# Turning q and k with VectorE and ScalarE in place of TensorE, 96x96 gram products among the convolutions, and a rotated order of attention's output channels

## The chip, the cores and the metric

The kernel runs on one core of a Trainium2 chip. The metric is device time in microseconds (us), from the first to the last instruction of the slowest core; here there is one core. The engines are TensorE (PE, matmuls, with its weight loads shown apart as PEld), VectorE (DVE), ScalarE (ACT), GpSimd (POOL) and SyncE (SP), which only issues transfers. Each engine works through its own queue in order, and semaphores make one wait for another. SBUF is the on-chip memory with 128 partitions; PSUM holds what TensorE writes, in banks.

## The reference

Two layers work on an image x of 384 channels and 192x192 pixels, in float32. The second (a 7x7 depthwise convolution after a group normalization) isn't touched by the change. The first is this, cut to what matters:

```
x1  = groupnorm(x)                                  # 32 groups
qkv = max over 2x2 pixels of (w_qkv @ x1 + b_qkv)   # 1152 channels, 96x96
qkv = depthwise 3x3 of qkv + b_dw
q, k, v = the three thirds, each as 8 heads of 48 channels x 9216 pixels
q, k = q, k divided by their norm over the pixels
attn = q @ k^T * temperature                        # 48x48 for each head
out  = sum over i of topk_softmax(attn, k_i) @ v * a_i,  k_i = 24, 32, 36, 38
x    = x + (w_proj @ upsample2x2(gelu(out)) + b_proj)
```

The attention is over channels: one 48x48 matrix for each head. Both q @ k^T (a sum over all pixels) and attn @ v are therefore products in which only the blocks of one head on the diagonal count.

## The kernel before

The channels lie on the partitions, in three tiles of 128 (`KT` = 3). A head has `HC` = 48 channels, so heads cross the borders of the tiles.

The q/k stage (lines 551 to 763) goes through the image in `NB` = 24 blocks of `PR` = 4 pooled rows. For each block and each of the six channel tiles of q and k, `pooled` multiplies the weights `wq` with the loaded rows (three groups of 512 columns, three matmuls of depth 128 each, L639) into one of the four PSUM buffers "pq", and VectorE takes the maximum over 2x2 pixels (L647) into a ring of rows, `ring`. `bordered` lets ScalarE copy a row of the ring to its other end (L669, L673), in two of three blocks. One block later, `depthwise` makes the 3x3 convolution with nine VectorE instructions (L680, L682) into a buffer `dst` of the pool `qkp`.

When all six tiles of a block are there, `products` (L688) does three things. ScalarE squares each tile and sums it into `ssq` (L691). TensorE transposes q and k, 128 pixels at a time, into the PSUM buffers "tr" (L700), because the sum over pixels needs pixels on the partitions, and ScalarE copies the result to SBUF as `qkT` (L706). TensorE then multiplies the turned q with the turned k into `grams`, one PSUM bank that collects the sum over all blocks (L709). `SPAN` says which columns of k meet the 128 q channels of a tile: 144, 192 and 144.

An fp32 matmul is two passes over the array, and the profile shows each pass with its weight load; a transpose is one pass.

What is between the q/k stage and the v stage: in the loop's last turn (`b == NB`) the first of 16 batches of v is convolved already (`convolve`, L530 to L549, PSUM buffers "pv"), with an `issue_after(multiplied)` that puts it behind a block's last gram product. Then `attention` (L769) scales the gram by the norms (L789), moves the heads' blocks with ten small transfers into `att` (L797), ranks and mixes the softmaxes on VectorE, spreads the result as blocks into `diag` (L851), transposes it and copies it to `attnT` (L862). Two further batches of v are convolved meanwhile.

The v stage runs over batches of 2 x 6 rows. For each, `attend` (L951) multiplies `attnT` with v: for each half and each tile `ct` of output channels, the tiles `dt` of v channels that share a head with it (`near`), seven products in all (L961), and ScalarE applies Gelu. `project` (L977) multiplies with `wp` (L985), whose rows are the channels of `gl` in the same order.

The order of instructions: the code is traced, and a planner puts each engine's queue in order, in order of the trace among those which its cost estimates hold ready. `keep(...)` fixes an instruction behind the last kept one of its engine; `issue_after(x)` puts what is traced inside it behind x on x's engine. A pool with `bufs=n` gives n buffers for each tag; a new tile waits until the old one's readers are done.

Of the kernel before, what the change touches and what calls it, by code (L numbers as in the profile page):

```python
# [8 lines left out]
F32 = mybir.dt.float32  # L9
AF = mybir.ActivationFunctionType  # L10
ALU = mybir.AluOpType
AX = mybir.AxisListType

P = 128
C = 384
KT = C // P
# [5 lines left out]
HC = C // HEADS  # L22
# [4 lines left out]
NB = PS // PR  # L27
IR = 2 * PR
BLK = IR * HW
PB = PR * PS  # L30
SUB = BLK // 512
NX = 3
GN_EPS = 1e-5


SPAN = []
for _mt in range(KT):
    _lo = (_mt * P) // HC * HC
    _hi = ((_mt + 1) * P - 1) // HC * HC + HC
    SPAN.append((_lo, _hi))  # L40

PIECES = []
for _mt in range(KT):
# [29 lines left out]
UT = 2  # L73
# [5 lines left out]
def conv_preact_d2(  # L79
# [17 lines left out]
    nc = tc.nc  # L97
# [16 lines left out]
    ident = const.tile([P, P], F32, name="ident")  # L114
# [31 lines left out]
    wp = const.tile([P, KT, C], F32, name="wp")  # L146
# [79 lines left out]

    ssq = const.tile([P, 2 * KT, NB], F32, name="ssq")
    attnT = const.tile([P, KT, C], F32, name="attnT")


    bctx = ExitStack()
# [26 lines left out]

    psx = ExitStack()
    pgram = psx.enter_context(tc.tile_pool(name="pgram", bufs=1, space=PSUM))  # L260
    gram = []
    for mt, (lo, hi) in enumerate(SPAN):
        o = sum(h - l for l, h in SPAN[:mt])
        gram.append((o, o + hi - lo))
    grams = pgram.tile([P, gram[-1][1]], F32, name="grams")
    gram = [grams[:, lo:hi] for lo, hi in gram]
    ptr = psx.enter_context(tc.tile_pool(name="ptr", bufs=3, space=PSUM))
    qx = ExitStack()
    pq = qx.enter_context(tc.tile_pool(name="pq", bufs=4, space=PSUM))
# [216 lines left out]
        w = wq[:, TWO, i * C : (i + 1) * C]  # L486
        nc.scalar.mul(w, w, rstd0[:, TWO : TWO + 1])
    with tc.issue_after(loaded):
        nc.sync.dma_start(wp, wprojT.rearrange("(t p) o -> p t o", p=P))

# [57 lines left out]

    with ExitStack() as bx:
        padp = bx.enter_context(tc.tile_pool(name="padp", bufs=1))
        qkp = bx.enter_context(tc.tile_pool(name="qkp", bufs=9))
        trp = bx.enter_context(tc.tile_pool(name="trp", bufs=2))

        gwp = bx.enter_context(tc.tile_pool(name="gwp", bufs=1))

# [66 lines left out]
        for ct in range(2 * KT):  # L624
            ring.append(padp.tile([P, 3 * PR + 2, PS + 2], F32, name=f"ring{ct}"))

        def pooled(b, ct, xb):
            rows = xb.rearrange("p t (r c) -> p t r c", c=HW)
            t = ring[ct]
            r0 = 1 + b % 3 * PR  # L630
            for g in range(3):
                begun, there = sums_qk.pop((b, ct, g), (None, False))
                ps = begun
                if not there:
                    ps = pq.tile([P, 512], F32, name=f"pq{b}_{ct}_{g}", tag="pq")
                    if begun is not None:
                        nc.scalar.copy(ps, begun)
                for kt in range(KT) if begun is None else (TWO,):
                    nc.tensor.matmul(  # L639
                        ps,  # L640
                        wq[:, kt, ct * P : (ct + 1) * P],
                        rows[:, kt, :, g * 64 : (g + 1) * 64],
                        start=(kt == 0),
                        stop=(kt == KT - 1),
                        skip_group_check=begun is not None,
                    )
                nc.vector.tensor_reduce(  # L647
                    t[:, r0 : r0 + PR, 1 + g * 32 : 1 + (g + 1) * 32],
                    ps.rearrange("p (h a w b) -> p h w a b", h=PR, a=2, b=2),
                    AX.XY,  # L650
                    ALU.max,
                )
# [32 lines left out]
            r0 = b % 3 * PR  # L685
            taps(dst, ct, lambda i, j: ring[ct][:, r0 + i : r0 + i + PR, j : j + PS])

        def products(b, qk):  # L688
            for i in range(2 * KT):
                junk = trp.tile([P, PB], F32, name=f"junk{b}_{i}", tag="junk")  # L690
                nc.scalar.activation(  # L691
                    junk, qk[i].rearrange("p h w -> p (h w)"), AF.Square,
                    accum_out=ssq[:, i, b : b + 1],
                )
            for j in range(PB // P):
                sides = []
                for s in range(2):
                    ps = ptr.tile([P, C], F32, name=f"tr{b}_{j}_{s}", tag="tr")
                    for i in range(KT):
                        nc.tensor.transpose(  # L700
                            ps[:, i * P : (i + 1) * P],
                            qk[s * KT + i].rearrange("p h w -> p (h w)")[:, j * P : (j + 1) * P],
                            ident,
                        )
                    sb = trp.tile([P, C], F32, name=f"qkT{b}_{j}_{s}", tag=f"qkT{s}")
                    nc.scalar.copy(sb, ps)  # L706
                    sides.append(sb)
                for mt, (lo, hi) in enumerate(SPAN):
                    last = nc.tensor.matmul(  # L709
                        gram[mt],  # L710
                        sides[0][:, mt * P : (mt + 1) * P],
                        sides[1][:, lo:hi],
                        start=False,
                        stop=(b == NB - 1 and j == PB // P - 1),
                        skip_group_check=True,
                    ).ins
            return last


        nc.tensor.matmul(  # L720
            grams, z[:, RUN : RUN + P], z[:, RUN : RUN + grams.shape[1]], start=True, stop=False,
            skip_group_check=True,
        )
        for b in range(NB + 1):
            xb = None
            if b < NB:
                xb = held.pop(b) if b in held else load_x(b, "xq")
            else:

                qx.close()  # L730
                pv = psx.enter_context(tc.tile_pool(name="pv", bufs=2, space=PSUM))
                xb = xpool.tile([P, 2 * UT, KT, RB * HW], F32, name="xv_begun", tag="xb")
                for kt in range(KT):
                    nc.sync.dma_start(xb[:, :, kt], image_rows(kt, order[0], 0, 2 * UT))
            qk = []
            for ct in range(2 * KT + 1):
                if b < NB and ct < 2 * KT:
                    if b == 0 and ct < 2:

                        if ct == 0:  # L740
                            pooled(b, 0, xb)
                            pooled(b, 1, xb)
                            biases()
                    else:
                        pooled(b, ct, xb)
                    bordered(b, ct)
                if b > 0 and ct > 0:
                    dst = qkp.tile([P, PR, PS], F32, name=f"qk{b}_{ct}", tag="qk")
                    qk.append(dst)
                    depthwise(b - 1, ct - 1, dst)  # L750
                    if ct == 2 * KT:
                        multiplied = products(b - 1, qk)
                    if b == NB:
                        with tc.issue_after(multiplied):
                            for n in ((), (), (0, 1), (), (2, 3), (4,), (5,))[ct]:
                                t0 = n // KT * UT
                                convolve(0, t0, n % KT, xb[:, t0 : t0 + UT], lambda ins: ins)
            if b == 2:
                for tiles in vrows:
                    row_borders(tiles)  # L760
            if b < len(pieces):
                with tc.issue_after(stats0):
                    weights(*pieces[b])

    xctx.close()

    near = {}

    def attention(ap):  # L769

# [13 lines left out]
        along_free(rkb, rn[:, KT : 2 * KT], ptr, "rk", "tr")  # L784
        yield

        scaled = ap.tile([P, KT, C // 2], F32, name="scaled")
        for mt, (lo, hi) in enumerate(SPAN):
            nc.vector.scalar_tensor_tensor(  # L789
                scaled[:, mt, 0 : hi - lo], gram[mt], rn[:, mt : mt + 1], rkb[:, lo:hi],  # L790
                ALU.mult, ALU.mult,
            )
        att = ap.tile([P, KT, HC], F32, name="att")
        for i, (mt, r0, r1, h) in enumerate(PIECES):
            eng = (nc.gpsimd, nc.scalar)[i % 2]
            o = h * HC - SPAN[mt][0]
            eng.dma_start(att[r0:r1, mt, :], scaled[r0:r1, mt, o : o + HC])  # L797
        yield


# [50 lines left out]
            eng.dma_start(diag[r0:r1, mt, h * HC : (h + 1) * HC], mix[r0:r1, mt, :])  # L851
        yield
        for dt in range(KT):
            cts = [ct for ct in range(KT) if SPAN[ct][0] < (dt + 1) * P and SPAN[ct][1] > dt * P]
            near[dt] = cts
            ps = ptr.tile([P, C], F32, name=f"aT{dt}", tag="tr")
            for ct in cts:
                nc.tensor.transpose(
                    ps[:, ct * P : (ct + 1) * P], diag[:, ct, dt * P : (dt + 1) * P], ident
                )  # L860
            lo, hi = cts[0] * P, (cts[-1] + 1) * P
            nc.vector.tensor_copy(attnT[:, dt, lo:hi], ps[:, lo:hi])  # L862

# [85 lines left out]
    def attend(i, pin=lambda ins: ins):  # L951
        b = order[i % NBC]
        vb = [vbs.pop((i, ct)).rearrange("p t c -> p (t c)") for ct in range(KT)]
        gl = gp.tile([P, KT, PBC], F32, name=f"gl{b}", tag="gl")
        for h in range(2):
            for ct in range(KT):
                dts = [dt for dt in range(KT) if ct in near[dt]]
                ps = ptr.tile([P, C], F32, name=f"po{b}_{ct}_{h}", tag="tr")
                for dt in dts:
                    keep(  # L960
# [563 lines left out]
```

## Time and profile before

| What | Value |
|---|---|
| Median of three runs | 2817.3 us (2817.22 to 2821.58) |
| Profiled execution | 2802.07 us, span 2800.4 us |
| TensorE clock granted, mean | 0.994 of full speed |
| Instructions on TensorE / VectorE / ScalarE / GpSimd | 8717 / 3383 / 1638 / 884 |
| Image moments and the first partial products | to about 190 us |
| q/k stage | to about 1355 us |
| Change of stage, attention | to about 1488 us |
| v stage | to about 2195 us |
| 7x7 convolution and output | to the end |

The profile is one execution. In a row of a group, the line number is followed by engine, operation and tiles (output <- inputs), the shapes, the count, then the total of busy time and the mean ns of one, and at the end the idle time of the engine just before these instructions, with what ended it. In a timeline row the first number is the start and the second how long the run of equal instructions lasted. In a table of stretches, each engine's busy us are followed by its count of instructions.

### The profile page before, as it was taken

Reading aid. Unit: us, or ns where it says so; the run is one execution under the profiler, and the core shown is the slowest. Engines: PE = TensorE matmul, PEld = TensorE weight load, DVE = VectorE, ACT = ScalarE, POOL = GpSimd, SP = SyncE. Lnnn points to the kernel's source line nnn. Section 1 sums busy time; section 2 is a strip of 40 time slices with the busy share of each in tenths; the row PEclk is TensorE's granted clock in tenths of the full one; section 3 lists DMA queues with packets and bytes.
Section 4 is the critical chain, followed back from the end, with each engine's and each line's share of the span. In section 5 each row is a group of like instructions: output and inputs, shape, how many; then the busy total and the mean of one; then the engine's idle time right before and its main releaser. Section 6 shows DMA issues by size and latency. Waiting matters only on the chain. (4 is left out here: it accounts for less than half of the span.)

```text
span 2800.4 us, 25638 instructions
## 1 busy us (share of the span) xinstructions
PE 2646.0 (94%) x8717; PEld 1588.6 (57%) x8717; DVE 2324.8 (83%) x3383; ACT 873.3 (31%) x1638; POOL 748.0 (27%) x884
## 2 busy tenths in 40 slices
PE   0399999999999999999999999999999899999998
PEld 0144444445445444444556666666666677777776
DVE  7989887887878878878798988889889678887786
ACT  0141111111111111111202232222323577777776
POOL 1023443100000000000102231010101477877777
PEclk9999999999999999999999999999999999999999
DMA  9976666401001001010235998575664899999998
GB/s 381 400 248 216 227 203 219 165 34 68 34 34 68 34 35 67 34 62 7 78 127 174 334 379 314 171 249 196 209 236 152 321 341 360 374 367 370 367 376 265
DMA packets 234002, 580.98 MB, mean 207 GB/s; under 512 B 16608, under 2 KB 165712, under 8 KB 217104
## 3 DMA queue, kind: packets, MB, share of 16 engines
q1 hardware_dynamic: 173376, 283.44, 28.8%
q0 software_dynamic: 37376, 148.85, 15.2%
q10 hardware_dynamic: 23120, 147.07, 14.0%
q8 instruction: 69, 1.13, 0.2%
q14 instruction: 61, 0.50, 0.0%
HBM read 370.93 MB, written 208.21 MB: 207 GB/s over the span
## 5 line engine op out<-in xcount | busy, mean ns | idle before, releaser
L639 PE MATMUL pq<-xq,wq 128*128 128x512 f32 x2268 | 990.7, 593 | 0.0
L639 PEld LDWEIGHTS pq<-xq,wq 128*128 128x128 f32 x2268 | 423.9, 190 | 491.3 <-issue 446.5
L682 DVE SCALAR_TENSOR_TENSOR qk<-ring,wd,qk 128x384 f32<-128x384 f32 x1152 | 674.8, 613 | 20.9 <-ACT ring L669 7.1
L537 PE MATMUL pv<-xv,wq 128*128 128x384 f32 x1656 | 539.8, 487 | 2.5 <-DVE rows L543 1.4
L647 DVE TENSOR_REDUCE ring<-pq 128x128 f32<-128x512 f32 x428 | 293.9, 688 | 193.5 <-PE pq L639 192.0
L1428 PE MATMUL pc<-main,w 128*128 128x288 f32 x1536 | 436.2, 407 | 3.9 <-POOL aux L1348 1.7
L537 PEld LDWEIGHTS pv<-xv,wq 128*128 128x128 f32 x1656 | 314.8, 190 | 218.6 <-DVE rows L543 3.0
L1448 DVE TENSOR_SCALAR apart<-pc,rb 32x576 f32<-32x576 f32 x384 | 312.2, 813 | 108.9 <-PE pc L1428 97.1
L1428 PEld LDWEIGHTS pc<-main,w 128*128 128x128 f32 x1536 | 290.8, 190 | 87.3 <-issue 2.1
L1446 ACT ACTIVATE apart<-pc,rb 32x576 f32<-32x576 f32 x384 | 281.1, 732 | 137.2 <-PE pc L1428 132.4
L905 DVE SCALAR_TENSOR_TENSOR vb<-rows,wd,vb 128x576 f32<-128x576 f32 x384 | 313.2, 817 | 11.2
L1428 PE MATMUL pc<-aux,h 128*128 128x288 f32 x768 | 249.5, 407 | 3.1 <-issue 2.4
L691 ACT ACTIVATE junk<-qk 128x384 f32<-128x384 f32 x144 | 75.3, 523 | 544.0 <-DVE qk L682 544.0
L1387 POOL COPY res<-apart 128x1152 f32<-128x1152 f32 (+1 forms) x96 | 218.4, 2305 | 48.6 <-DMA out_dram<-res 40.2
L773 POOL TENSOR_TENSOR rn<-rn,halfpos 128x6 f32<-128x6 f32 x1 | 1.4, 1360 | 850.6 <-DVE rn L772 850.6
L1022 DVE TENSOR_TENSOR sx<-xr,y 128x576 f32<-128x576 f32 x180 | 203.7, 1173 | 26.9 <-ACT y L993 21.2
L1063 POOL DMA_DIRECT2D sd<-sx x96 | 72.2, 755 | 491.8 <-DVE sx L1022 472.6
L543 DVE TENSOR_REDUCE rows<-pv 128x192 f32<-128x768 f32 x144 | 137.8, 957 | 55.7 <-PE pv L537 55.6
L1428 PEld LDWEIGHTS pc<-aux,h 128*128 128x128 f32 x768 | 145.6, 190 | 45.2 <-issue 4.4
L1042 ACT ACTIVATE wq<-sx,negmid 128x1152 f32<-128x1152 f32 x96 | 120.6, 1256 | 95.4 <-DVE sx L1022 91.2
L1271 DVE SCALAR_TENSOR_TENSOR w<-eye,sb,w 128x512 f32<-128x512 f32 x96 | 144.1, 1540 | 1.5
L985 PE MATMUL pr<-gl,wp 128*128 128x288 f32 x576 | 142.6, 407 | 0.0
(226 smaller groups left out, 2113.6 us busy)
## 6 DMA issues: line engine op xcount, KB each, us to landing
sd<-sx POOLq DMA_DIRECT2D x96, 600.0 KB, 9.9
out_dram<-res SPq DMA_DIRECT2D x192, 288.0 KB, 10.7
main<-sd ACTq DMA_DIRECT2D x46, 1200.0 KB, 5.1
xv<-in_x_dram SPq DMA_DIRECT2D x138, 384.0 KB, 6.5
xr<-in_x_dram SPq DMA_DIRECT2D x45, 1152.0 KB, 12.0
xq<-in_x_dram SPq DMA_DIRECT2D x21, 2304.0 KB, 8.2
w<-wt ACTq DMA_DIRECT2D x46, 1024.0 KB, 6.9
xs<-in_x_dram SPq DMA_DIRECT2D x24, 1536.0 KB, 15.6
```

Of the source, the lines that this page charges most:

```text
L537: nc.tensor.matmul(ps[:, u, 0 : RB * HW], wq[:, kt, o : o + P], xb[:, u, kt, :], start=(kt == 0), stop=(kt == KT - 1),)
L639: nc.tensor.matmul(ps, wq[:, kt, ct * P : (ct + 1) * P], rows[:, kt, :, g * 64 : (g + 1) * 64], start=(kt == 0), stop=(kt == KT - 1), skip ...
L647: nc.vector.tensor_reduce(t[:, r0 : r0 + PR, 1 + g * 32 : 1 + (g + 1) * 32], ps.rearrange("p (h a w b) -> p h w a b", h=PR, a=2, b=2), AX. ...
L682: nc.vector.scalar_tensor_tensor(dst, src, w, dst, ALU.mult, ALU.add)
L905: pin(nc.vector.scalar_tensor_tensor(dst, src, w, dst, ALU.mult, ALU.add))
L985: nc.tensor.matmul(ps[:, 0:H], wp[:, ct, ot * P : (ot + 1) * P], gl[:, ct, h * H : (h + 1) * H], start=(ct == 0), stop=(ct == KT - 1),)
L1022: nc.vector.tensor_tensor(bass.AP(flat.tensor, flat.offset + at(e) + a * RUN, [flat.ap[0], [JP, NT], [1, NJ], [at(f) - at(e), 2]],), xq[:, ...
L1271: nc.vector.scalar_tensor_tensor(mid, eye.unsqueeze(1).to_broadcast([P, 4, P]), sb[:, c : c + 1], mid, ALU.mult, ALU.add,)
L1387: keep(copy(res[ps, k], apart[ps, :, k].rearrange("p e n -> p n e")))
L1428: nc.tensor.matmul(ahead[q][:, k, 0 : NT * NJ], lhs, rhs, start=(j == 0), stop=(j == 2), skip_group_check=True,)
L1446: keep(nc.scalar.mul(dst, src, scale))
L1448: keep(nc.vector.tensor_scalar_mul(dst, src, scale))
```

## The change

In the q/k stage, each tile that `depthwise` has finished is transposed by VectorE in squares of 32x32, in place in the grid of squares (`nc.vector.transpose`, 128x384, into `turns`). When the three tiles of q (or of k) are there, ScalarE puts the squares in their places: `turned` makes 16 copies for each side, from one quadrant of 32 partitions to another, 32x288 elements each; two of four rounds are traced at once and the other two after the next tile's transpose. The squares for the norms write their unused output to a "tr" buffer in PSUM.

The gram is made of pairs of heads: four products of 96x96 for each 128 pixels, twelve a block. They are traced one after each convolution product (`pinned`, `between`): the products of block b-2 begin with channel tile 3 of block b, and from block 2 on the convolution products are kept in the written order. In the loop's last turn they stand among the first products of v, and those of the last block follow when all else is traced. `qkp` goes from 9 to 5 buffers, `trp` from 2 to 1.

In `attention`, one multiplication of 96x384 scales the gram by k's norms, and after the small transfers another, 128x144, scales it by q's.

For v, the output channels of attention are rotated by 96 (`TURN`): tile 0 holds channels 96 to 223, tile 1 channels 224 to 351, tile 2 channels 352 to 383 and 0 to 95. Each tile then shares heads with two tiles of v (`MEET`), six products where there were seven. `attnT` is cleared at the start, since only the heads' blocks are copied into it, and `wp` is loaded in the rotated order with three transfers.

```diff
+PAIR = 2 * HC
+TURN = PAIR
+MEET = [[dt for dt in range(KT) if any(
+    (TURN + ct * P + j) % C // HC in range(dt * P // HC, ((dt + 1) * P - 1) // HC + 1)
+    for j in range(P))] for ct in range(KT)]
...
+    nc.gpsimd.memset(attnT, 0.0)
...
-        nc.sync.dma_start(wp, wprojT.rearrange("(t p) o -> p t o", p=P))
+        nc.sync.dma_start(wp[:, 0:whole], ...)
+        nc.sync.dma_start(wp[0:over, whole], wprojT[C - over :])
+        nc.sync.dma_start(wp[over:P, whole], wprojT[0:TURN])
...
-        qkp = bx.enter_context(tc.tile_pool(name="qkp", bufs=9))
-        trp = bx.enter_context(tc.tile_pool(name="trp", bufs=2))
+        qkp = bx.enter_context(tc.tile_pool(name="qkp", bufs=5))
+        trp = bx.enter_context(tc.tile_pool(name="trp", bufs=1))
...
+        def pinned(ins):
+            if ins.ins.engine != mybir.EngineType.PE:
+                return ins
+            keep(ins)
+            while between and next(between[0], between) is between:
+                between.pop(0)
+            return ins
...
+                    if b > 1:
+                        pinned(ins)
...
+        def squares(b, ct, t):
+            junk = ptr.tile([P, C], F32, name=f"junk{b}_{ct}", tag="tr")
+            nc.scalar.activation(junk, t, AF.Square, accum_out=ssq[:, ct, b : b + 1])
+
+        def turned(side, turns):
+            for a in range(P // Q):
+                for f in range(P // Q):
+                    nc.scalar.copy(
+                        side[f * Q : (f + 1) * Q].rearrange("p c (t n) -> p t c n", n=P)[
+                            :, :, :, a * Q : (a + 1) * Q
+                        ],
+                        turns[a * Q : (a + 1) * Q].rearrange("p t (c n) -> p t c n", n=P)[
+                            :, :, :, f * Q : (f + 1) * Q
+                        ],
+                    )
+                yield
...
-                    for i in range(KT):
-                        nc.tensor.transpose(
...
-                    nc.scalar.copy(sb, ps)
...
+                for lo in range(0, C, PAIR):
+                    multiplied = keep(
+                        nc.tensor.matmul(
+                            grams[0:PAIR, lo : lo + PAIR],
+                            sides[0][:, j, lo : lo + PAIR],
+                            sides[1][:, j, lo : lo + PAIR],
...
+                if ct == (KT if b < NB else 1) and done:
+                    between.append(products(b - 2, done))
...
                     depthwise(b - 1, ct - 1, dst)
...
+                    nc.vector.transpose(turns[:, t], flat)
+                    squares(b - 1, ct - 1, flat)
+                    for _ in copies:
+                        pass
+                    if t == KT - 1:
+                        side = trp.tile([P, PB // P, C], F32, name=f"qkT{b}_{s}", tag=f"qkT{s}")
+                        sides.append(side)
+                        copies = turned(side, turns)
+                        for _ in range(2):
+                            next(copies)
                     if b == NB:
-                        with tc.issue_after(multiplied):
...
+                            convolve(0, t0, n % KT, xb[:, t0 : t0 + UT], pinned)
+                        if ct == 2 * KT:
+                            for _ in copies:
+                                pass
+                            between.append(products(b - 1, sides))
+                            for left in between:
+                                for _ in left:
+                                    pass
...
-            nc.vector.scalar_tensor_tensor(
-                scaled[:, mt, 0 : hi - lo], gram[mt], rn[:, mt : mt + 1], rkb[:, lo:hi],
+        nc.vector.tensor_tensor(scaled[0:PAIR], grams[0:PAIR], rkb[0:PAIR], ALU.mult)
...
+            for l, h in ((lo, min(hi, TURN)), (max(lo, TURN), hi)):
+                if l < h:
+                    o = (l - TURN) % C
+                    nc.vector.tensor_copy(attnT[:, dt, o : o + h - l], ps[:, l:h])
...
-                dts = [dt for dt in range(KT) if ct in near[dt]]
+                dts = MEET[ct]
```

## The prediction

> **What bounds the kernel now.** I first read the busy shares, then the busy time by stage, because the whole-run shares mix four stages with different limits.
>
> ```profile
> PE 2646.0 (94%) x8717; PEld 1588.6 (57%) x8717; DVE 2324.8 (83%) x3383; ACT 873.3 (31%) x1638; POOL 748.0 (27%) x884
> ```
>
> ```profile
> core 0: us, PE busy (x) PEld busy (x) DVE busy (x) ACT busy (x) POOL busy (x), PEclk, DMA share, GB/s
> 300.00:1300.00 1000.00, 998.96 (x2802) 481.22 (x2801) 802.29 (x1407) 144.55 (x432) 94.33 (x151) 1.00 0.24 87
> 1355.00:1393.00 38.00, 35.93 (x159) 24.12 (x158) 24.50 (x47) 9.13 (x26) 4.96 (x6) 1.00 0.28 94
> 1500.00:2130.00 630.00, 628.85 (x2149) 408.61 (x2148) 554.66 (x639) 174.56 (x381) 96.95 (x130) 1.00 0.72 251
> 2130.00:2200.00 70.00, 59.32 (x224) 43.60 (x223) 62.68 (x67) 36.80 (x86) 14.48 (x20) 0.91 0.73 259
> ```
>
> In the q/k stage (300 to 1300) and in the v stage (1500 to 2130) TensorE is busy 99.8% of the time. VectorE is at 80% and 88%, ScalarE at 14% and 28%, and the DMA engines have room. So the stages that the change touches are paced by TensorE. The chain of work that ended last says nothing here: it names only the output stage.
>
> Next come the groups of the q/k stage and TensorE's own timeline around one block of four rows, where starts can be subtracted (a "busy" time includes the modelled drain of each matmul).
>
> ```profile
> L682 DVE SCALAR_TENSOR_TENSOR qk<-ring,wd,qk 128x384 f32<-128x384 f32 x937 | 551.7, 614 | 19.5 <-ACT ring L669 7.1
> L647 DVE TENSOR_REDUCE ring<-pq 128x128 f32<-128x512 f32 x354 | 243.9, 689 | 177.7 <-PE pq L639 176.4
> L706 ACT COPY qkT<-tr 128x384 f32<-128x384 f32 x114 | 52.5, 477 | 118.7 <-PE tr L700 99.4 <-PE grams L709 17.4
> ```
>
> ```profile
> 1304.48 1.50 PE L700 MATMUL tr<-ident,qk 128*128 128x128 f32 x10
> 1305.82 1.02 PE L639 MATMUL pq<-xq,wq 128*128 128x512 f32 x2
> ...
> 1308.95 1.79 PE L709 MATMUL grams<-qkT,qkT 128*128 128x144 f32 x12
> 1310.58 0.49 PE L700 MATMUL tr<-ident,qk 128*128 128x128 f32 x3
> 1310.90 1.02 PE L639 MATMUL pq<-xq,wq 128*128 128x512 f32 x2
> 1311.76 1.01 PE L709 MATMUL grams<-qkT,qkT 128*128 128x144 f32 x6
> 1312.61 43.08 PE L639 MATMUL pq<-xq,wq 128*128 128x512 f32 x100
> 1355.53 2.15 PE L700 MATMUL tr<-ident,qk 128*128 128x128 f32 x13
> ```
>
> The reader sees one full block, 1304.48 to 1355.53, 51.05 us. A convolution pass (an fp32 matmul is two passes) takes 42.92/100 = 0.429 us; 108 of them make 46.35 us. What is left, 4.69 us, is 18 transposes (0.107 each where they run in threes, 2.21 us in all) and 18 gram passes (1.63 + 0.85 = 2.48 us). VectorE waits for TensorE (176 us before its reduces), not the other way round.
>
> For the v stage the same view gives the price of an attention pass: 28 of them from 1538.92 to 1545.71, 0.2425 us each.
>
> ```profile
> 1538.92 6.95 PE L961 MATMUL po<-vb,attnT 128*128 128x288 f32 x28
> 1545.71 11.78 PE L537 MATMUL pv<-xv,wq 128*128 128x384 f32 x36
> ```
>
> **What the Trainium skill says.** "TensorE: Matmul & The Clock Gate", section "LDWEIGHTS (loading the stationary operand)": the load time goes with the number of weight columns, P/1.2 ns, whatever the depth. The trace agrees for 128 columns: the 30 one-column bias passes (176.71 to 179.98) take 0.109 us each, against 0.107. By that, 96 columns load in an estimated 0.080 us. "VectorE: DVE Perf Modes", section "The three transpose paths": VectorE turns 32x32 squares only, 311 ns for 128x128 bf16. "ScalarE: Activation LUTs", section "What ACT_TABLE_LOAD costs": a ScalarE instruction with immediates takes 186 ns + 0.833 ns per element, and neighbours overlap by 93 ns. The trace agrees roughly: 96-element copies take 272 ns (266 by the page), 384-element copies from PSUM 477 ns (506).
>
> **The change part by part.**
> *TensorE, q/k.* Per block 18 transposes go: 2.21 us. The gram becomes 12 products of 96x96 in place of 9 of 128x144 or 128x192: 24 passes. Moving 96 columns costs 96/512 x 0.429 = 0.081 us a pass, 0.161 a product, and its own weights load in the same 0.080 us. The 128-column weights of the convolution pass that follows need 0.109 us beside a 0.081 us pass, so 0.028 us may show: 0.19 us a product, 2.3 us a block. Bounds: 1.93 (all loads hidden, as they are between transposes and convolutions now) and 4.6 (both loads exposed at the 190 ns of a weight-load row). I take 2.3: saving 4.69 - 2.30 = 2.39 us a block. 22 blocks' grams lie ahead of the end of the last q/k convolution: 22 x 2.39 = 52.6 us.
>
> *VectorE, q/k.* Six transposes of 128x384 a block. No row shows one. The skill's 311 ns for 128 elements plus 256 more at the 0.96 GHz of the same page is an estimated 0.58 us; without that fixed part, the 0.49 us of the one-input row L680; above, twice the estimate if fp32 ran at half rate, 1.15 us. I take 0.58: 3.5 us a block. VectorE now works 0.802 x 51.05 = 41.0 us a block; 44.5 of a new period of 48.7 us. It is hidden under TensorE with 4 us to spare; the four "pq" buffers give about 10 us of slack in order.
>
> *ScalarE, q/k.* Six copies of 477 ns go; 32 copies of 32x288 come, 426 ns by the page (333 from start to start), 10.7 to 13.6 us a block. The squares stay, writing to PSUM. From 7.4 us now, ScalarE goes to some 18 of 48.7 us. Hidden. Behind these copies in its queue stand the squares, which free the "qk" buffers (five, 40 us of taps), and the ring-row copies of L669/L673, which VectorE needs one channel tile later; a copy ahead of them delays them by 0.4 us each, and VectorE has waited only 7 us for them in 1000.
>
> *The new wait.* Convolution products now stand in written order, and each product of block b-2 stands between two of them, from channel tile 3 of block b. The first waits for the last ScalarE copies of block b-2's k side. Taps end some 6 us into block b, 16 copies take 5.3 us: ready at about +12, wanted at +24. Cost nothing; half a block covers it. Queued behind it are all convolutions, and behind these VectorE's reduces. Single buffers of the turned sides: the next q side is written after the last product, some 13 us into ct 3; ScalarE waits, nobody behind it is urgent.
>
> *The end of the stage.* From the last q/k convolution (1355.53) to the first convolution of the second v batch (1392.99) is 37.5 us now. After it: k side of block 22 ready at +9 (taps 3, transpose 0.6, copies 5.3), until which TensorE idles behind its first product; then 72 v passes of 0.3225 us and 12 products, 25.5 us: +34. VectorE's rest (15.5 us of taps now, some 5 us of lead that it no longer builds up, 2 us of transposes, 5 of reduces) ends near +30, then 5.9 us of transpose and copies, then 2.3 us of products: +38.5. The idle time may lower the clock for a while (0.91 in the stretch above that has 3.6 us waits): I take +42.5, a loss of 5 us; bounds -3 and +14. The softmax chain then starts some 8 us later, with 10 us in hand before the first attention pass at 1488.57. The extra multiply of 128x144 (0.3 us) lies on it.
>
> *v stage.* Six instead of seven products per half: 4 passes less per batch, 0.97 us. 13 batches in the TensorE-bound loop: 12.6 us. In the last three TensorE waits for others (3.6, 1.1, 3.7 us), so half of 2.9: 1.4. Together 14.0; bounds 11 and 15.5.
>
> *At nothing:* clearing attnT (about 1 us of GpSimd in a start bound by DMA until 136 us), two more wp transfers on the SP queue near 144 us (0.45 us each; the next block load issues at 194, wp is used at 1507), copies of attnT in five pieces for three (under 1 us, inside the 10 us).
>
> Sum: -52.6 + 5 - 14.0 = -61.6 us, 2802.1 to 2740.5 in the profiled execution (span 2800.4). The median of the runs, 2817.3, is 15.2 above that execution; I take the same difference off it: 2756.
>
> **The rivals.**
> *A, the forecast:* TensorE stays the bound. Its own range, from the bounds above but not all at once: 2741 to 2772. Chance 0.60.
> *B, VectorE eats part of it.* fp32 transposes at 1.15 us bring VectorE to 47.9 of 48.7 us; reduces come late, "pq" runs out, and a block takes about 50: 22 x 1.05 = 23, with +5 - 14: 2785. For it: VectorE is the second-busiest engine and gets more work. Against: a transpose that cost this much would be double the nearest row. 0.18.
> *C, the products cost what the old ones and the transposes did*, 4.6 us a block, their loads exposed between convolutions: 2 + 14 - 5: 2806. Against: now no load shows between transposes and convolutions. 0.07.
> *D, slower:* a product at the head of TensorE's fixed order waits for ScalarE's copies in each block. At 5 us a block, 22 x (5 - 2.39) - 14 + 5 = +48: 2866. It turns the sign at (52.6 + 9)/22 = 2.8 us a block, that is, if the copies come 15 us later than I put them, or cost over (48.7 + 2.8 - 4.6)/32 = 1.46 us each. For it: nothing else can run on TensorE then. Against: no ACT row of this size is above 0.73 us. 0.13.
>
> **How the numbers follow.** The remaining 0.02 is a larger gain. Within 0.2% (5.6 us) is about what a measurement of this kernel can't tell from no change; part of C and the edge of B fall there, 0.03. Faster 0.84, slower 0.13. The range 2738 to 2802 holds A, B and most of C, and leaves out D and the larger gain.
>
> **What would show it.** Right: no L700 row; a block period near 48.7 us with TensorE still above 99% between 300 and 1250; gram passes of about 0.09 us; VectorE near 91%; transposes near 0.6 us; 384 attention passes, batches of 49.4 us for 50.35. Wrong: TensorE waiting for ScalarE's qkT copies at the gram line, or for VectorE's reduces at the convolution line; transposes over 1 us; copies over 1 us; a gap of more than 10 us after the last q/k convolution.

## The result

The changed kernel takes 2786.3 us (median of four runs, 2778.0 to 2791.6) where the kernel before takes 2817.3 (also the median of four): ratio 0.9882, 95% interval 0.9859 to 0.9905, or 31 us less. That is about half of the forecast 61 us, on the forecast side and inside the range. A repetition, in which the kernel before ran in 2800.0 us, gave 0.9872 (0.9853 to 0.9892), 34.6 us less.

The busy shares of the profile after, and its stretches of time, with the change of stage from 1300 on:

```profile
PE 2591.1 (93%) x8365; PEld 1525.2 (55%) x8365; DVE 2456.2 (88%) x3527; ACT 1140.1 (41%) x2262; POOL 746.7 (27%) x885
```

```profile
300.00:1300.00 1000.00, 994.56 (x2686) 454.65 (x2685) 930.26 (x1590) 371.58 (x965) 90.84 (x146) 1.00 0.24 84
1300.00:1340.00 40.00, 25.56 (x70) 12.44 (x69) 37.20 (x71) 19.07 (x50) 0.00 (x0) 0.79 0.00 0
1500.00:2130.00 630.00, 602.99 (x2030) 387.17 (x2028) 542.05 (x616) 167.24 (x365) 91.87 (x123) 0.98 0.74 251
2130.00:2200.00 70.00, 60.86 (x234) 46.44 (x234) 60.30 (x80) 40.01 (x89) 15.50 (x25) 0.90 0.71 247
```

TensorE is still the busiest engine of the q/k stage, but no longer without gaps (99.5% against 99.9%), VectorE is at 93%, and there are now two places where TensorE stands: the change of stage (busy 25.6 of 40 us, with a mean clock of 0.79) and, in this profile, the v stage (busy 603 of 630 us). The groups that the change added, and the weight loads of the convolution, of the stretch 300 to 1250:

```profile
L725 ACT COPY qkT<-turns 32x288 f32<-32x288 f32 x608 | 260.4, 428 | 14.2 <-DVE turns L791 7.2
L741 PE MATMUL grams<-qkT,qkT 128*96 128x96 f32 x470 | 77.7, 247 | 0.0
L741 PEld LDWEIGHTS grams<-qkT,qkT 128*96 128x96 f32 x471 | 76.8, 163 | 118.9 <-issue 118.9
L663 PEld LDWEIGHTS pq<-xq,wq 128*128 128x128 f32 x2077 | 373.7, 190 | 399.7 <-issue 329.8 <-DVE ring L673 50.0 <-DVE qk L708 14.6
L791 DVE STREAM_TRANSPOSE turns<-qk 128x384 f32<-128x384 f32 x116 | 66.2, 571 | 0.9
```

Placing copies of 428 ns, transposes of 571 ns: what the forecast took for one instruction, 426 and 580. TensorE's timeline shows the products between the convolutions:

```profile
256.47 1.05 PE L663 MATMUL pq<-xs,wq 128*128 128x512 f32 x2
257.35 0.33 PE L741 MATMUL grams<-qkT,qkT 128*96 128x96 f32 x2
257.52 1.05 PE L663 MATMUL pq<-xs,wq 128*128 128x512 f32 x2
258.41 0.33 PE L741 MATMUL grams<-qkT,qkT 128*96 128x96 f32 x2
```

A product takes 0.17 us from start to start, and the convolution product behind it 0.88 to 0.89 where two passes make 0.86: 0.20 us in all, 0.19 forecast. The first products of successive blocks start at 256.30, 305.01, 353.72, 402.43: 48.71 us apart, the 48.7 of the forecast. But later blocks are longer.

Where the time is, as points on TensorE's timeline (us from the start; the difference to the line above in brackets):

| Point | Before | After | After, repeated |
|---|---|---|---|
| end of the last q/k convolution | 1355.7 | 1316.4 | 1313.0 |
| first convolution of the second v batch | 1393.0 (37.3) | 1364.1 (47.7) | 1360.1 (47.0) |
| first attention product | 1488.6 (95.6) | 1464.2 (100.1) | 1459.8 (99.7) |
| thirteenth batch's attention product | 2094.7 (606.1) | 2083.8 (619.5) | 2053.4 (593.7) |
| first product of the 7x7 convolution | 2219.1 (124.5) | 2209.3 (125.6) | 2179.4 (126.1) |
| end of the span | 2800.4 (581.3) | 2784.9 (575.6) | 2754.3 (574.9) |

The lines behind the change of stage, the first of the kernel before and the others of the changed one, first profile:

```profile
1392.99 7.90 PE L537 MATMUL pv<-xv,wq 128*128 128x384 f32 x24
1303.30 13.07 PE L663 MATMUL pq<-xq,wq 128*128 128x512 f32 x30
1364.11 11.78 PE L549 MATMUL pv<-xv,wq 128*128 128x384 f32 x36
```

The last stage isn't touched by the change. It takes 574.7 to 579.0 us in the eleven other profiles of this study, the kernel with the v part alone among them (577.0), and 581.3 us in the one profile of the kernel before; why that one is longer isn't shown. For the rest, the repeated run reads: 42.7 us gained in the q/k stage, 13.8 lost between it and the first attention product, 12.4 gained in the twelve v batches, 1.6 lost behind them, 39.7 in all. In the first profile the v batches lost 13.5 instead.

Three readings name the places. VectorE's wait for ring rows in the q/k stage, in the list of waits from 300 to 1250. The first line is of the kernel before, the others are of the changed one:

```profile
DVE qk L682 <- ACT ring L669: 6.8, 20, 0.3
PEld pq L663 <- DVE ring L673: 50.0, 95, 1.6
DVE qk L708 <- ACT ring L695: 31.1, 31, 2.3
```

And two places of ScalarE's and VectorE's timeline, 34 us apart:

```profile
1176.49 6.61 ACT L725 COPY qkT<-turns 32x288 f32<-32x288 f32 x15 [0.41 <-DVE turns L791]
...
1183.43 1.93 DVE L708 SCALAR_TENSOR_TENSOR qk<-ring,wd,qk 128x384 f32<-128x384 f32 x3 [2.03 <-ACT ring L695]
...
1210.20 7.02 ACT L725 COPY qkT<-turns 32x288 f32<-32x288 f32 x16
...
1214.88 0.69 DVE L673 TENSOR_REDUCE ring<-pq 128x128 f32<-128x512 f32 x1
1217.25 0.38 ACT L520 ACTIVATE ring<-ones,negb 128x98 f32<-128x98 f32 x1
1217.53 0.25 ACT L695 COPY ring<-ring 128x96 f32<-128x96 f32 x1
1217.82 1.93 DVE L708 SCALAR_TENSOR_TENSOR qk<-ring,wd,qk 128x384 f32<-128x384 f32 x3 [2.26 <-ACT ring L695]
```

The planner issued both halves of a side's copies in one go (at the first place all but one of them). At the second place the ring row was ready when VectorE's reduce ended (1215.6), but its copy stood behind sixteen placing copies, and VectorE, in order, stood for 2.26 us with the next reduces behind it. From 442 us on, two such waits of some 2 us come in every three blocks, twelve in all; before the change there is none over 0.3 us. TensorE's own waits, at the change of stage and in the v stage:

```profile
1322.97 1.65 PE L549 MATMUL pv<-xv_begun,wq 128*128 128x384 f32 x2 [6.61 <-DVE ring L673]
1332.45 0.64 PE L741 MATMUL grams<-qkT,qkT 128*96 128x96 f32 x2 [7.84 <-ACT qkT L725]
...
1654.80 1.62 PE L549 MATMUL pv<-xv,wq 128*128 128x384 f32 x2 [15.88 <-DMA xv<-in_x_dram]
```

### The profile page after: what moved, and what is told of

The parts are those of the page before. It is cut to its first block, busy times and chain, and to the rows that moved or that the text cites. A ratio compares the mean times of both kernels' runs of the same rounds, so it can differ in the third digit from the quotient of the medians.

```text
span 2784.9 us, 25837 instructions
## 1 busy us (share of the span) xinstructions
PE 2591.1 (93%) x8365; PEld 1525.2 (55%) x8365; DVE 2456.2 (88%) x3527; ACT 1140.1 (41%) x2262; POOL 746.7 (27%) x885
## 5 line engine op out<-in xcount | busy, mean ns | idle before, releaser
L663 PE MATMUL pq<-xq,wq 128*128 128x512 f32 x2268 | 1028.8, 597 | 5.4 <-DVE ring L673 4.7
L708 DVE SCALAR_TENSOR_TENSOR qk<-ring,wd,qk 128x384 f32<-128x384 f32 x1152 | 699.4, 616 | 59.5 <-ACT ring L695 32.1
L663 PEld LDWEIGHTS pq<-xq,wq 128*128 128x128 f32 x2268 | 408.7, 190 | 437.3 <-issue 364.0
L549 PE MATMUL pv<-xv,wq 128*128 128x384 f32 x1656 | 545.7, 490 | 26.0 <-DMA xv<-in_x_dram 21.7
L725 ACT COPY qkT<-turns 32x288 f32<-32x288 f32 x768 | 329.0, 428 | 20.7 <-DVE turns L791 9.3
L1441 POOL COPY res<-apart 128x1152 f32<-128x1152 f32 (+1 forms) x96 | 222.0, 2338 | 13.3 <-ACT apart L1500 9.5
L741 PEld LDWEIGHTS grams<-qkT,qkT 128*96 128x96 f32 x576 | 92.8, 165 | 147.3 <-issue 136.1
## 6 DMA issues: line engine op xcount, KB each, us to landing
xr<-in_x_dram SPq DMA_DIRECT2D x45, 1152.0 KB, 11.7
```

The source lines that it names most:

```text
L549: nc.tensor.matmul(ps[:, u, 0 : RB * HW], wq[:, kt, o : o + P], xb[:, u, kt, :], start=(kt == 0), stop=(kt == KT - 1),)
L663: ins = nc.tensor.matmul(ps, wq[:, kt, ct * P : (ct + 1) * P], rows[:, kt, :, g * 64 : (g + 1) * 64], start=(kt == 0), stop=(kt == KT - 1) ...
L708: nc.vector.scalar_tensor_tensor(dst, src, w, dst, ALU.mult, ALU.add)
L725: nc.scalar.copy(side[f * Q : (f + 1) * Q].rearrange("p c (t n) -> p t c n", n=P)[:, :, :, a * Q : (a + 1) * Q], turns[a * Q : (a + 1) * Q ...
L1441: keep(copy(res[ps, k], apart[ps, :, k].rearrange("p e n -> p n e")))
```

## The experiments

The theory after the result: TensorE's saving is all there; what is missing is ScalarE's queue order in the q/k stage (some 12 us) and a longer chain of taps, transposes, copies and products at the end of it (some 10 us more than forecast). The rivals: VectorE at 93% simply has too much work; the DMA engines take back what the v stage gains. Ratios are to the kernel before, on the same chip.

**The v part alone.** The kernel before with `MEET`, `TURN`, the cleared `attnT` and the rotated `wp`; its core is

```diff
-                dts = [dt for dt in range(KT) if ct in near[dt]]
+                dts = MEET[ct]
```

> The kernel before with the v part of the change alone (rotated channels, six products, attnT cleared and copied by heads, wp in three transfers). Theory 1: the v part is worth 12 to 14 us by itself (0.97 us for each of 13 batches in the TensorE-bound loop, a little after it), so about 2803 on 2817, ratio 0.995. Theory 2: batches 1 to 4, which also write the halos, are bound by the DMA engines, so that their 4 us turn into a wait of TensorE for xv loads: 8 to 10 us in all, with more than 3 us of TensorE waiting for xv between the first and the fifth attention product.

Measured: 0.9967 (0.9956 to 0.9978), 9.3 us less. Its batches with the lowered count take 49.38 us from start to start, as in the changed kernel:

```profile
1542.42 5.98 PE L984 MATMUL po<-vb,attnT 128*128 128x288 f32 x24
1591.80 5.98 PE L984 MATMUL po<-vb,attnT 128*128 128x288 f32 x24
```

That is 0.97 us less than before in each batch, as forecast; TensorE's waits for xv are 1.6 us (1.1 in the kernel before), not 3 or more. So theory 2 lacks its wait, and the time moved less than the 12 of theory 1, but the twelve batches between the first and the thirteenth attention product gained 11.0 us (595.1 against 606.1). The last three batches gained nothing (124.6 us from the thirteenth batch to the 7x7 convolution, 124.5 before): the step that booked 1.4 us there was wrong.

**The q/k part alone.** The changed kernel, without the two transfers of wp that have nothing left to load, and with

```diff
-TURN = PAIR
+TURN = 0
```

> The changed kernel with TURN = 0, so that v keeps seven products and its old order of channels; the q/k part alone. From the trace of the changed kernel: the last q/k convolution ends 39 us earlier than before, the change of stage costs 15 us more, so -24 us if nothing else happens: about 2793, ratio 0.991. If starting the v stage earlier only runs into the DMA engines there, the gain is smaller, 0 to 10 us, and TensorE waits 15 to 25 us for xv loads around batch 5.

Measured: 0.9893 (0.9873 to 0.9912), 27.9 us less. The last q/k convolution ends at 1316.8, the second v batch starts 47.5 us later, and TensorE has no wait for xv of its own between the first and the thirteenth attention product (1.2 us in the weight loads). So starting the v stage earlier did not run into the DMA engines in this execution. The two parts roughly add: 9.3 and 27.9 are 37.2, the whole is 34.6 in one measurement and 31.0 in the other.

**ScalarE's copies in the written order.** `keep` on the ring-row copies and on the placing copies:

```diff
-                nc.scalar.copy(t[:, 3 * PR + 1, row], t[:, 1, row])
+                keep(nc.scalar.copy(t[:, 3 * PR + 1, row], t[:, 1, row]))
...
-                    nc.scalar.copy(
+                    keep(nc.scalar.copy(
                         side[f * Q : (f + 1) * Q]...
```

> The changed kernel with ScalarE's ring-row copies and its placing copies held in the written order, so that a ring row's copy stands between the first eight and the last eight placing copies of a side and no sixteen run in one go. Theory 1 (the 12 us that the q/k stage fell short come from VectorE waiting for ring rows behind a run of sixteen copies in every third block): blocks of 50.3 us become 48.7 to 49.2, VectorE's wait for L695 falls from 31 to under 15 us, the last q/k convolution ends some 8 to 12 us earlier. Theory 2 (VectorE simply has too much work in those blocks): blocks stay at 50.3, the time within 2 us of the changed kernel.

Measured: 0.984 (0.9826 to 0.9853), 44.0 us less. The last q/k convolution ends at 1304.7, 11.7 us ahead of the changed kernel's first profile and 8.3 ahead of its repetition. The waits for ring rows fell by a third only, from 31.1 to 21.0 us, less than theory 1 wanted; TensorE's wait for the reduces behind them went from 50 to 20 us in the weight loads and from 4.7 to 0.8 in the products. The trace shows why so few waits had to go: only one side's copies were divided, and the other side's sixteen still run in one go, with a ring row behind them.

```profile
1198.10 7.02 ACT L725 COPY qkT<-turns 32x288 f32<-32x288 f32 x16
...
1205.72 1.27 DVE L708 SCALAR_TENSOR_TENSOR qk<-ring,wd,qk 128x384 f32<-128x384 f32 x2 [2.26 <-ACT ring L695]
```

This is the second of the two waits shown above, and TensorE does not stand behind it here: from block 10 on, every block takes 48.71 us. So VectorE's idle time covers one wait of 2 us in three blocks, but not two within 34 us. Of the 12.3 us that the blocks of the changed kernel were too long, 2.8 are left. The table of stretches, for the changed kernel (repeated) and for this one:

```profile
300.00:1250.00 950.00, 945.30 (x2555) 432.22 (x2554) 882.30 (x1508) 354.76 (x923) 94.81 (x148) 1.00 0.26 90
```

```profile
300.00:1250.00 950.00, 949.17 (x2579) 438.24 (x2578) 892.31 (x1522) 356.44 (x930) 95.12 (x149) 1.00 0.26 91
```

VectorE is busier (892 of 950 us), and TensorE stands less. So in the blocks with long waits the order of ScalarE's queue decided, not VectorE's load alone. One thing the experiment doesn't hold still: in every third block the planner also moved some of VectorE's own instructions, and what that did by itself is not shown.

**Less transposing.** One column of squares instead of twelve, the rest of the copied squares zeros:

```diff
-                    nc.vector.transpose(turns[:, t], flat)
+                    nc.vector.transpose(turns[:, t, 0:Q], flat[:, 0:Q])
```

> The changed kernel in which VectorE transposes one column of squares (128x32) of each tile in place of 128x384; the other squares that ScalarE places are zeros, so most of the gram is left out. 0.57 us becomes some 0.2, 2.2 us less of VectorE's work a block, all waits as they were. Theory 1 (the wait for ring rows behind sixteen copies holds up the q/k stage): the last q/k convolution ends only a few us earlier, 1310 to 1316. Theory 2 (VectorE's load does): blocks of 50.3 us vanish, it ends near 1303. If VectorE's lag also sets the change of stage, the 47.7 us from there to the second v batch shrink by 4 to 7 us.

Measured: 0.9903 (0.9887 to 0.992), 28.5 us less: slower than the changed kernel. Neither theory expected that; the last q/k convolution ended at 1326.0, 10 to 13 us later. VectorE had less to do, 833 us of the 950 from 300 to 1250, and TensorE waited more. The list of waits there:

```profile
PEld pq L666 <- DVE ring L676: 70.3, 99, 3.0
DVE qk L709 <- ACT junk L722: 48.5, 19, 3.7
DVE qk L711 <- ACT ring L698: 34.1, 40, 3.3
```

and one place of its timeline:

```profile
622.65 7.90 ACT L728 COPY qkT<-turns_all 32x288 f32<-32x288 f32 x18
...
630.57 0.27 ACT L698 COPY ring<-ring 128x96 f32<-128x96 f32 x1
...
630.88 1.92 DVE L711 SCALAR_TENSOR_TENSOR qk<-ring,wd,qk 128x384 f32<-128x384 f32 x3 [3.28 <-ACT ring L698]
```

With other durations the planner made other runs of copies, here eighteen in a row, and both the ring rows and the squares that free "qk" buffers stood behind them. So the experiment changed the order along with the load. It shows that this order (ring-row waits of 3.3 us) costs more than the saved work brings; it can't say what less work would bring in an equal order.

**Block 22's products later at the change of stage.**

```diff
-                if ct == (KT if b < NB else 1) and done:
+                if ct == (KT if b < NB else 4) and done:
```

> The changed kernel with block 22's products among v's third and fourth convolution of the change of stage, in place of the first and second. Theory 1 (TensorE's wait of 7.8 us behind the first product, and the lowered clock after it, delay everything behind): the 7.8 us wait goes and the second v batch starts 6 to 10 us earlier, 2778 to 2780. Theory 2 (the last block's taps, transposes and copies set the end of the stage anyway): TensorE waits the same 5 to 8 us ahead of the last twelve products, and the time is within 2 us of the changed kernel's.

Measured: 0.987 (0.9856 to 0.9883), 36.1 us less, where the changed kernel had 34.6 and 31.0 in other measurements. The 7.84 us wait is gone, but the second v batch starts 45.5 us after the last q/k convolution, 1.5 to 2.2 us sooner than in the changed kernel: the wait moved to the last block's own products, ahead of which TensorE now stands for 4.7 us in three pieces, 2.8 of them for ScalarE's copies. Theory 2 holds.

**Both reorderings.** The two edits together.

> The changed kernel with ScalarE's ring-row and placing copies in the written order and with block 22's products later. The first alone was worth 8 us of the time (11.7 us at the last q/k convolution), the second 1 to 2 us at the change of stage. If they add, 45 us less than before, ratio 0.983 to 0.984; the last q/k convolution ends near 1305, the second v batch starts 44 to 46 us after it.

Measured: 0.9824 (0.9805 to 0.9843), 50.6 us less, 5 more than if they added. Every block after the first takes 48.71 us, with TensorE busy 950.0 of the 950 us from 300 to 1250 and VectorE 891.9, though one ring-row wait of 2 us in three blocks is left here too. The change of stage takes 41.5 us, shorter than the two reorderings' own gains would make it (some 44 us), and its timeline shows what is last there:

```profile
1327.52 7.04 ACT L725 COPY qkT<-turns 32x288 f32<-32x288 f32 x16 [1.96 <-PE grams L741]
...
1335.19 7.03 ACT L725 COPY qkT<-turns 32x288 f32<-32x288 f32 x16
...
1342.27 3.71 PE L741 MATMUL grams<-qkT,qkT 128*96 128x96 f32 x22 [1.13 <-ACT qkT L725]
```

The last block's q side is placed only after block 22's last product has read the one buffer (ScalarE's queue stood 1.96 us for it), its k side 7 us after that, and the last products wait for it.

**Two buffers for the turned q side**, on top of both reorderings:

```diff
-                        side = trp.tile([P, PB // P, C], F32, name=f"qkT{b}_{s}", tag=f"qkT{s}")
+                        side = trp.tile([P, PB // P, C], F32, name=f"qkT{b}_{s}", tag=f"qkT{s}", bufs=2 - s)
```

> The kernel with both reorderings (ScalarE's copies in the written order, block 22's products later) and two buffers for the turned q side. In the kernel with both reorderings ScalarE began to place the last block's q side only when block 22's last product had read the buffer, and TensorE waited 7 us at the end for ScalarE's 32 last copies. Theory 1 (the single buffer is late): the q side is placed as soon as its squares are there, 4 to 6 us earlier, and the 41.5 us from the last q/k convolution to the second v batch become 36 to 38. Theory 2 (VectorE's last taps are late, and the copies follow them anyway): 41 to 42 us as before.

Measured: 0.9793 (0.9778 to 0.9808), 2738.7 us against 2797.6, 58.9 us less: the fastest kernel of the study, and nearly the gain that was forecast. The change of stage takes 35.1 us, 2.2 less than before the change:

```profile
1319.07 3.51 ACT L725 COPY qkT<-turns 32x288 f32<-32x288 f32 x8
1323.31 3.51 ACT L725 COPY qkT<-turns 32x288 f32<-32x288 f32 x8
1329.51 7.05 ACT L725 COPY qkT<-turns 32x288 f32<-32x288 f32 x16
...
1336.61 2.11 PE L741 MATMUL grams<-qkT,qkT 128*96 128x96 f32 x22 [0.19 <-ACT qkT L725]
```

The q side is placed 8 us earlier, while block 22's products still run. Theory 1 holds. In the q/k stage the copies run in eights here, no ring-row wait is over 0.4 us, and the last q/k convolution ends at 1304.0, where it ended at 1304.3 with one wait of 2 us in three blocks: those waits cost nothing.

**GpSimd takes half of the last block's copies**, on top of that:

```diff
+                    copy = nc.gpsimd.tensor_copy if last and f % 2 else nc.scalar.copy
-                    keep(nc.scalar.copy(
+                    keep(copy(
...
-                        copies = turned(side, turns)
+                        copies = turned(side, turns, b == NB)
```

> The same with two q buffers, and half of the last block's 32 copies done by GpSimd, which is idle then. If ScalarE's run of copies at the end (7.0 us for sixteen) is what TensorE's last products wait for, GpSimd's share takes 3 us off it, unless a copy of 32x288 takes GpSimd more than 0.9 us: 34 to 36 us from the last q/k convolution to the second v batch, and 46 to 48 us less than the kernel before in all, ratio 0.982.

Measured: 0.9799 (0.9779 to 0.9818), the same as without it within the intervals; the change of stage takes 36.5 us, so the 3 us did not come. GpSimd's copies take 424 ns (median), as long as ScalarE's, and in the last run eight of each go side by side in 3.5 and 3.7 us; GpSimd's eight before that took 5.3 us. But VectorE's last taps came later in this order (k's squares at 1336.6, 27 us after the last q/k convolution; 25 us in the kernel above), so ScalarE's last run of copies was no longer what was late by itself.

Its q/k stage ended at 1309.2, 5.3 us later than in the kernel above. Its first block was 1.9 us shorter than there, but blocks 3 to 7 were 7.5 us too long, although no ring row was more than 0.4 us late there: TensorE waited for VectorE's reduces. The stretch 380 to 430 of this kernel and of the one above:

```profile
380.00:430.00 50.00, 47.43 (x130) 21.65 (x129) 48.16 (x77) 18.58 (x49) 25.77 (x40) 1.00 0.63 204
```

```profile
380.00:430.00 50.00, 50.00 (x136) 23.13 (x135) 47.94 (x83) 18.72 (x49) 21.06 (x31) 1.00 0.63 206
```

VectorE is busy some 48 of 50 us there in both, so in the early blocks its load has nothing in hand and can hold TensorE up by itself. Why it did so in one of these kernels and not in the other is not shown.

**The changed kernel again, and with fewer transfers.** The first profile's wait of TensorE for xv, 21.7 us around batch 5, was in no forecast.

> The changed kernel itself, a second time. Theory 1 (the 21.7 us that TensorE waited for xv loads around batch 5 in the changed kernel's profile belong to that execution, whose transfers were slower, not to the change): the wait is 0 to 6 us here, the profile's span some 2763 where before's is 2800, and the ratio 0.985 to 0.988. Theory 2 (the change brings the first batches into the DMA engines' limit): the wait is 15 to 25 us again.

Measured: 0.9872 (0.9853 to 0.9892), span 2754.3 us in the profile. TensorE waits 1.7 us for xv, weight loads included; in the first profile these are 21.7 and 8.1 us, partly the same time. In the repeated run's table of stretches the DMA engines moved

```profile
1550.00:1600.00 50.00, 50.00 (x171) 32.30 (x170) 45.41 (x52) 13.77 (x30) 18.76 (x25) 1.00 1.03 385
```

where the first profile has

```profile
1550.00:1600.00 50.00, 50.00 (x171) 32.30 (x170) 45.52 (x52) 13.77 (x30) 18.52 (x26) 1.00 1.03 371
1600.00:1640.00 40.00, 38.92 (x136) 25.46 (x134) 36.42 (x44) 8.94 (x21) 11.63 (x16) 1.00 1.03 359
```

The DMA share is the same 1.03 in both, that is, the engines are full; the same code got 385 GB/s in one execution and 359 to 371 in the other. Whether that goes with the execution or with the chip isn't shown. An earlier start of the v stage is not enough for a wait: TensorE's products waited 5.8 us for xv with ScalarE's copies divided and 6.9 us with both reorderings, but only 2.0 us with two buffers, where the v stage begins earliest.

The other kernel uses batch 1's image rows again for the residual of batches 2 to 4, three times 3.5 MB less:

```diff
+        if i in (2, 3, 4):
+            return kept_r[ot]
...
+        if i == 1:
+            kept_r[ot] = xr
```

> The changed kernel without the residual's loads of batches 2, 3 and 4 (batch 1's image rows are used again, so the sum is wrong there): 10.4 MB less in the stretch in which the DMA engines are full. If those transfers are what TensorE waits for around batch 5, the wait is 0 here whatever it is in the changed kernel on the same chip, and the difference of the two times is that wait; with no wait there, both times agree within 2 us.

Measured: 0.9853 (0.9831 to 0.9875), 2758.0 us against 2765.4 for the changed kernel on that chip, and no wait for xv in its profile (span 2754.6, as long as the changed kernel's without the wait). The 7 us between the medians are near the scatter of the runs (2756.0 to 2766.0 and 2750.7 to 2764.1). So the stretch of batches 1 to 5 has no DMA time in hand, and one profiled execution lost some 20 us there. Since the kernel before has the same transfers, and its runs in the first measurement lie 11 to 20 us above its profile, in which TensorE waits 1.1 us for xv, it may have lost time there too; no profile here shows it.

## Why the forecast was half right

*TensorE's saving in q/k.* Right in mechanism and size: 0.20 us a product against 0.19, blocks of 48.71 us against 48.7 wherever nobody else was late, no L700 row. By the Trainium skill's "TensorE: Matmul & The Clock Gate", section "LDWEIGHTS (loading the stationary operand)", a load's time goes with its columns, an estimated 27 ns less for 96 than for 128. The trace agrees: 163 ns in the row of the 96-column load, 190 in that of the 128-column load. With the runs of copies divided, the q/k stage ends at 1304 to 1305 in three kernels, 51 us earlier, and at 1309 in a fourth; 52.6 were forecast. Rival C is refuted.

*VectorE hidden, with 4 us to spare.* The load was right (571 ns against 580 for a transpose; 93% against 91%) and rival B, a bound by VectorE's load in every block, fell: in the kernel with both reorderings it runs at 94%, and TensorE has no gap from 300 to 1250. The margin is thin, though, and in the early blocks there is none (7.5 us lost in the kernel with GpSimd). The step that failed is the one after it, that a placing copy ahead of a ring row's copy "delays them by 0.4 us each". It priced one copy; the planner put fifteen or sixteen there, 6.6 to 7.0 us, and VectorE stood for 2 us twice in three blocks. The forecast's "4 us to spare" in a block covered one of these waits, but not the second, 34 us later, with reduces behind it. Nine of the blocks after the first three were 0.5 to 2.4 us longer than 48.71, 12.3 us in all, most of the 13.3 us between the forecast's 52.6 and the 39.3 of the first profile.

*The new wait of TensorE on the copies (rival D).* Not in the q/k stage: the products wait nowhere there, half a block covered them. But once, at the change of stage, 7.84 us. The forecast had this wait and the lowered clock, but put its end at +9, where it came at +16: it did not see that the first v product needs the banks of "pq" and so the last reduce of a VectorE that is behind (6.61 us).

*The end of the stage, +5 us.* Mis-sized: +10.4, and another 4.5 until the first attention product, where "10 us in hand" was to hide it: VectorE's reduces of v came late behind the softmax work (TensorE waited 3.6 us for them at 1379, 1.4 us at a like place before). Two terms were too small: sixteen copies take 7.0 us, not 5.3, since they don't overlap; and the q side's single buffer, of which the forecast said "nobody behind it is urgent", was urgent in the last block: a second one shortens the change of stage by 6.4 us.

*v stage, -14 us.* 0.97 us a batch is exact. It came 12 times between the points above, 11.0 to 12.4 us; the 1.4 us from the last batches did not come, since TensorE waits for others there anyway.

*From one profiled execution to the median.* The forecast took the same 15 us off both. The two profiles of the changed kernel differ by 31 us (2784.9 and 2754.3), 26 of them in the v batches, where TensorE waited for transfers, mostly in the first one. That is as much as the whole gain in the medians, so a single profile is to be compared stage by stage, and the whole time by the runs.

## What to carry to other kernels

Work that is hidden by its engine's load isn't hidden by its engine's queue: price a moved instruction as the whole run that a planner may issue at once, and ask who else is served by that queue; here ScalarE was busy 37% of the time and still held VectorE up. A wait need not vanish to stop costing: one of two was enough. Where an in-order engine serves two users, fix the order of the short urgent pieces against the long patient ones, and give the last turn of a loop its own look: a single buffer that costs nothing in the steady state was worth 6 us at the end. The three edits together, the order of the copies, the later products and the second buffer, brought 58.9 us, nearly the forecast gain.

## What was not expected of the hardware

- Placing copies don't overlap. Sixteen of 32x288, SBUF to SBUF between quadrants, take 7.02 to 7.05 us, 0.44 us from start to start at 428 ns each. The Trainium skill's "ScalarE: Activation LUTs", section "What ACT_TABLE_LOAD costs", says that ACTIVATE instructions back to back overlap by about 93 ns. The trace agrees for ACTIVATEs: 18 fills of borders at the change of stage, 342 ns each, take 4.50 us, 0.25 from start to start. The forecast took the overlap for the copies too, which the page doesn't name; these COPY instructions don't overlap. Whether the kind of instruction or the change of quadrant is the reason wasn't tried.
- GpSimd makes the same copy in 424 ns (median of 16, up to 660), as fast as ScalarE.
- A VectorE transpose of fp32 takes 0.57 us for 128x384 and 0.20 us for 128x32, so about one ns for each further element of a partition; the half rate that rival B asked for, 1.15 us, did not show.
